# A macaron block with two routed expert layers on one core: expert products with the weights as the fixed side, and expert tiles sorted in one more class

## The chip, the cores and the metric

One core of one Trainium2 chip runs the whole program. The metric is the device time of the program in microseconds (us); the time of a kernel is the median of its runs.

## The reference, cut to what matters

2048 tokens (8 sequences of 256) with 128 features pass six stages, each added to what came in; all in float32. Stages one and three are the same expert layer:

```python
normed = _rmsnorm(x, norm_weight)                       # x is a layernorm of the stream
probs = softmax(normed @ router_weight.T)
topk_w, topk_idx = top_k(probs, 2); topk_w = topk_w / sum(topk_w)
for e in range(8):
    gate, up = split(normed @ gate_up_weight[e].T)      # 352 columns each
    out_e = (silu(gate) * up) @ down_weight[e].T
    moe_out = moe_out + combine[..., e, None] * out_e
return x + alpha * moe_out
```

Between them lies causal attention with 16 heads of 8. Behind them come a token-shift network (called mix here), a gated sum of nine shifted copies of the values (shift), and mix again.

## The kernel before, in words

The stream lies in SBUF as four tiles `x[0]` to `x[3]`, one for each group of 512 tokens (4 x 128 tokens on partitions, 128 features). All work is stated in Python as operations of the class `Work`: an engine, an estimated time, what it needs, and which buffers it takes and frees. `Work.issue` then places all of them by a list schedule and records each engine's instructions in that order, so the order on every engine is fixed by the planner's estimates and by the biases `BIAS` (added to the rank of late groups). `InOrder.issue` records each instruction, so nearly all of them show line 63 in the profile, and a register load shows line 72. Where the planner expects PE to idle, it places warming matmuls `pw`.

An expert layer (`moe_layer`) goes like this:

- `moe_route`, per group: normalise, store the rows to device memory (`rows0`, `rows1`), transpose, multiply by the router, take the top two (`topmost`).
- `moe_plan`, twice per layer: first over groups 0 and 1 alone, then over all groups. It counts tokens per expert with small matmuls and computes on DVE which row goes to which slot. There are 39 tiles of 128 slots; each tile has one expert. The first 9 tiles (`few`) are whole tiles of one expert filled from groups 0 and 1 alone; the 30 others come from the second plan. The plan leaves `take` (which row each slot fetches), `slot` (where a token's two results lie) and `expert` (the expert of each tile).
- `moe_experts` and `moe_tile`, per tile: POOL gathers 128 rows by an indirect DMA (`xs`), up to four tiles share a transpose `pt` and a scaled copy `nT`. PE reads the tile's expert into a register (`number`), then multiplies `nT` (the fixed side) with 352 columns of `gu` picked by the register, once for the gate (`pg`) and once for the up half (`pu`). ACT takes silu (`sg`), DVE multiplies (`hid`), PE transposes `hid` in three pieces (`ph`, at columns 0, 128 and 224: the list `HC`), ACT copies that (`hT`), and three matmuls with the expert's down weights add up to `po`. DVE copies it (`ys`), and SP stores it.
- `moe_back`, per group: for each of a token's two experts, four indirect DMAs on POOL fetch the results (`back`), and DVE adds them to `x`. Groups 0 and 1 may start once tiles 0 to 23 are stored; groups 2 and 3 once all 39 are.

All matmul results share eight PSUM banks (tag `b`). The attention's masks and constants (`mask_q`, `mask_k`, `va`, `mpad`, `onerow`) are made once the first layer's `affined` operation is done. In the second layer the end of the expert tiles is interleaved with mix of groups 0 and 1; shift and the last mix of all groups follow.

Of the kernel before, what the change touches and what calls it, by code (L numbers as in the profile page):

```python
# [19 lines left out]
P = 128  # L20
NG = 4
# [14 lines left out]
BIAS = (25.0, 30.0, 40.0, 55.0, 20.0, 2.0, -6.0)  # L36
# [181 lines left out]
def tile_macaron(ctx: ExitStack, tc: tile.TileContext, a: dict, out: bass.AP):  # L218
# [64 lines left out]
    with nc.allow_low_precision("zeros and ones"):  # L283
# [49 lines left out]
            "b": 8, "xs": 3, "nT": 3, "y": 2, "nTr": 1, "sg": 2, "hid": 2, "hT": 2, "ys": 4,  # L333
# [120 lines left out]
    def moe_layer(n, first):  # L454

        few = 2 * GT * first - 7
        r = {
            "n": n, "first": first, "few": few, "stored": {}, "all_stored": {}, "topped": {},
            "plan": {}, "hold": {},
        }  # L460
        for name, shape, dtype in (
            ("top", [P, NT, 8], F32), ("which", [P, NT, 8], U32), ("w", [P, NT, 2], F32),
            ("ab", [P, 2, NT], F32), ("rs", [P, NT], F32), ("slot", [P, 2 * NT], U32),
            ("take0", [P, few], U32), ("take1", [P, TILES - few], U32), ("expert", [1, TILES], I32),


            ("end", [P, E], F32), ("full", [P, 2, E], F32), ("base", [P, E], F32),
            ("both", [P, E], F32),
        ):
            r[name] = ctile(f"{name}_{n}", shape, dtype)  # L470
        for name, rows in (
            ("rows0", GT * first * P), ("rows1", NT * P), ("ys", TILES * P),
        ):
            r[name] = dram.tile([rows, P], F32, name=f"{name}_{n}", tag=f"{name}_{n}")
        return r

    def moe_route(g, r):
# [29 lines left out]
        tag = "nTr" if r["n"] else "nT"  # L507
        b1, b2, nTb = Buf("b"), Buf("b"), Buf(tag)
        pt = w.pe(0.44, lambda: transposed(filled[0].out), *filled, uses=[y], takes=[b1], spare=1)

        def scale_rows():
            nT = wtile(tag, "nT", (P, GT * P))
            nc.scalar.activation(
                nT, pt.out.rearrange("p t d -> p (t d)"), AF.Copy, scale=norm_w
            )
            return nT
# [85 lines left out]
    def moe_plan(r, whole):  # L602


        few = r["few"]
# [6 lines left out]
        def small(name, shape, dtype=F32):  # L612

            sizes = dict(zip("abc", shape[1:]))
            wide = 2 * NT * (TILES - 9)
            width = dict(
                oh=2 * NT * E, m=NT * E, slot=NT * E, past=2 * NT * E, sums=P, hit=wide, val=wide,
                le=3 * E, ef=1, eg=1, cb=E, nr=2 * E, at2=2 * E, up=2 * E,
                until=3 * E, whole=E,
            ).get(name, 2 * NT)  # L620
            rows = 1 if shape[0] == 1 else P
            room = wk.tile([rows, width], dtype, tag=name, name=name, bufs=1)
            n = 1
            for m in shape[1:]:
                n *= m
            v[name] = room[0 : shape[0], 0:n]
            if len(sizes) > 1:
                v[name] = v[name].rearrange(
                    f"p ({' '.join(sizes)}) -> p {' '.join(sizes)}", **sizes
                )  # L630
            return v[name]
# [34 lines left out]
        def place():  # L666

            sums = v["sums"]
            pp = bank([P, nt + 1, E], "pp")
            nc.tensor.matmul(  # L670
                pp[:, nt, :], lhsT=sums, rhs=same_e[0 : nt * E], start=True, stop=True
            )
            flat = pp.rearrange("p t e -> p (t e)")[:, 0 : nt * E]
            nc.tensor.matmul(flat, lhsT=before, rhs=v["m"], start=True, stop=False)
            nc.tensor.matmul(
                flat, lhsT=sums, rhs=earlier[0 : nt * E, 0:nt, :].rearrange("p t e -> p (t e)"),
                start=False, stop=True,
            )
            return pp
# [26 lines left out]
        def all_ends():  # L706
# [4 lines left out]
            left = small("cb", [P, E])  # L711
            nc.vector.tensor_tensor(left, placed.out[:, nt, :], full[:, 0, :], ALU.subtract)
            nc.vector.tensor_scalar(left, left, 63.5, 1.0 / P, ALU.add, ALU.mult)
            nc.vector.tensor_scalar(left, left, ROUND, ROUND, ALU.add, ALU.subtract)
            nr = small("nr", [P, 2, E])
            nc.vector.tensor_scalar(nr[:, 0, :], left, 1.0, None, ALU.min)
            nc.vector.tensor_tensor(nr[:, 1, :], left, nr[:, 0, :], ALU.subtract)

            until = small("until", [P, 3, E])
            nc.vector.tensor_copy(until[:, 0, :], r["end"])  # L720
            for k in range(2):
                nc.vector.tensor_tensor_scan(
                    until[:, k + 1, :], one8, nr[:, k, :], until[:, k, E - 1 : E], ALU.mult, ALU.add
                )


            at2 = small("at2", [P, 2, E])
            nc.vector.tensor_tensor(at2, until[:, 1:3, :], nr, ALU.subtract)
            up = small("up", [P, 2, E])
# [3 lines left out]
            nc.vector.tensor_tensor(up[:, 1, :], at2[:, 1, :], at2[:, 0, :], ALU.subtract)  # L733
            nc.vector.tensor_scalar(up[:, 1, :], up[:, 1, :], -1.0, float(P), ALU.add, ALU.mult)

        def all_slots():
            each, twice = [P, nt, E], [P, nt, 2, E]
# [3 lines left out]
                r["full"].unsqueeze(1).to_broadcast(twice), ALU.is_ge,  # L741
# [3 lines left out]
            nc.vector.tensor_tensor(past[:, :, 0, :], past[:, :, 0, :], past[:, :, 1, :], ALU.add)  # L745
            nc.vector.tensor_tensor(slot, slot, past[:, :, 0, :], ALU.add)

        ended = w.dve(2.4 if whole else 0.9, all_ends if whole else ends, placed, uses=[bp])
        spotted = w.dve(
            1.7 if whole else 0.75, all_slots if whole else slots, ended, uses=[bp]  # L750
# [73 lines left out]
        def which_expert():  # L824
# [3 lines left out]
            m = E * (3 if whole else 1)  # L828
# [34 lines left out]
    def moe_experts(r, sizes):  # L863


        stored, numbers, pus, turned, downs = [], {}, [], [], []
        k0 = 0
        for h in range(2):
            plan = r["plan"][h]
            rows = r["all_stored" if h else "stored"].values()  # L870
            for n in sizes[h]:
# [15 lines left out]
                for j in range(n):  # L887
                    got.append(w.pool(
                        0.98, lambda h=h, k=k0, j=j, f=gather: f(h, k, j), plan["taken"], *rows,
# [19 lines left out]
                for j in range(n):  # L909
                    stored.append(  # L910
                        moe_tile(r, plan, k0 + j, nT, nb, j, pus, turned, downs, numbers)
                    )
# [6 lines left out]
    def moe_tile(r, plan, k, nT, nb, j, pus, turned, downs, numbers):  # L919
        bg, bu, bh, bo = (Buf("b") for _ in range(4))  # L920
        sb, hb, tb, yb = Buf("sg"), Buf("hid"), Buf("hT"), Buf("ys")

        def number():
            numbers[k] = nc.tensor.value_load(
# [3 lines left out]
        known = w.pe(0.03, number, plan["experts"], *pus[-2:-1], lag=0.8)  # L928

        def product(c):  # L930
            wt = gu[:, bass.ds(numbers[k], 1), :].rearrange("p o h -> p (o h)")
            out = bank([P, HID], "pg" if c == 0 else "pu")
            nc.tensor.matmul(
                out, lhsT=nT.out[:, bass.ts(j, P)], rhs=wt[:, HID * c : HID * (c + 1)],
                start=True, stop=True,
            )
            return out

        pg = w.pe(0.6, lambda: product(0), known, nT, weights, *pus[-1:], *turned[-2:-1], *downs[-3:-2],
                  takes=[bg], uses=[nb], spare=3)  # L940
        pu = w.pe(0.6, lambda: product(1), pg, takes=[bu], uses=[nb])
        pus.append(pu)

        def gate():
            sg = wtile("sg", "sg", (P, HID))
# [7 lines left out]
        sg = w.act(0.47, gate, pg, takes=[sb], uses=[bg])  # L953

        def gated():
            hid = wtile("hid", "hid", (P, HID))
# [8 lines left out]
        hid = w.dve(0.53, gated, sg, pu, takes=[hb], uses=[sb, bu, bg])  # L965

        def turn():
            ph = bank([P, len(HC), P], "ph")
            for c, c0 in enumerate(HC):
                nc.tensor.transpose(ph[:, c, :], hid.out[:, c0 : c0 + P], ident)  # L970
            return ph

        ph = w.pe(0.34, turn, hid, takes=[bh], uses=[hb])
        turned.append(ph)

        def keep():
            hT = wtile("hT", "hT", (P, len(HC), P))
            nc.scalar.copy(hT, ph.out)
            return hT

        hT = w.act(0.48, keep, ph, takes=[tb], uses=[bh])

        def down():
            po = bank([P, P], "po")
            wt = dw[:, bass.ds(numbers[k], 1), :, :].rearrange("p o c d -> p (o c) d")
            for c in range(len(HC)):
                nc.tensor.matmul(
                    po, lhsT=hT.out[:, c, :], rhs=wt[:, c, :], start=(c == 0),
# [4 lines left out]
        po = w.pe(0.67, down, hT, takes=[bo], uses=[tb])  # L993
# [14 lines left out]
    def moe_back(g, r, stored):  # L1008
# [3 lines left out]
        until = 2 * GT * r["first"] + E if g < r["first"] else TILES  # L1012
# [10 lines left out]
        for c in range(2):  # L1023
# [3 lines left out]
            def gather(t, c, box=box):  # L1027
                if t == 0:
# [9 lines left out]
                    0.98, lambda t=t, c=c, f=gather: f(t, c), plan["slots"], *stored[:until],  # L1038
# [21 lines left out]
    def attention(begun):  # L1060
# [6 lines left out]
        def constants(mask, step):  # L1067
# [8 lines left out]
            w.pool(1.3, lambda m=m, step=step: constants(m, step), begun)  # L1076
# [8 lines left out]
            ), begun,  # L1085
# [3 lines left out]
            [w.pool(1.4, lambda v=v: nc.gpsimd.memset(v[:, :, :, DK:32], 1.0), begun)] for v in va  # L1089
# [3 lines left out]
            [[w.pool(0.5, lambda m=m: nc.gpsimd.memset(m, 0.0), begun)] for m in row]  # L1093
# [550 lines left out]
    outs = attention(r0["hold"][0]["affined"])  # L1644
# [94 lines left out]
```

## Time and profile before

| what | value |
|---|---|
| median of 5 runs | 588.6 us (588.47 to 595.54) |
| profiled execution, its own time | 590.61 us |
| its span | 588.9 us |
| mean granted clock of PE | 0.933 |
| busy: PE, weight loads, DVE, ACT, POOL | 514.4, 363.8, 320.4, 253.7, 229.2 us |

The profile is of one execution. PE is TensorE, PEld its weight loads (they overlap its matmuls), DVE is VectorE, ACT ScalarE, POOL GpSimd, SP the engine that issues plain DMAs. In the slices, each digit is the busy share of a fortieth of the span in tenths, and PEclk the granted clock in tenths. A row of the groups has the busy time and the mean of one instruction, then the idle time of the engine ahead of it and what ended it ("issue" is a wait for nothing that the profile shows, "remote" one for an unknown source). A row of the timeline has the start, the length, the engine and the operation. A row of the windows has the stretch, its length, then busy time (and instructions) of PE, PEld, DVE, ACT and POOL, the granted clock, the DMA share and GB/s. Ends of matmuls are modelled.

In time: loading, routing and the first plan of layer one to about 34 us; its tiles to about 176, the last of them beside attention, which runs from about 131 to 335; the tiles of layer two from 335 to 484; then the back-gathers and the tail of shift and mix to 589.

### The profile page before, as it was taken

To read this page: it belongs to the slowest core of one execution; us is meant where nothing else is said; L and a number is where in the kernel's file an instruction comes from. 1 tells how busy PE (TensorE), PEld (TensorE's weight loads), DVE (VectorE), ACT (ScalarE), POOL (GpSimd) and SP (SyncE) were. 2 spreads that over 40 slices of the span, in tenths; PEclk is the share of its full clock that TensorE was granted. 3 is DMA by queue.
4 is the path that set the end of the run, shared out by engine and by line. 5 is a ranking of instruction groups with operands and counts; after the bars stand their busy time and mean duration, and the time that the engine had idled before them with its cause. 6 is when DMAs were issued, how large, how long until landed. Compare 5 with 4: busy or idle time off the path is not lost.

```text
span 588.9 us, 12554 instructions
## 1 busy us (share of the span) xinstructions
PE 514.4 (87%) x4619; PEld 363.8 (62%) x4619; DVE 320.4 (54%) x1139; ACT 253.7 (43%) x536; POOL 229.2 (39%) x239
## 2 busy tenths in 40 slices
PE   7869599887997899999998799597985999699985
PEld 3447478655774666776776575475764774466574
DVE  7676144245853586777772378132323344479891
ACT  3223166324153246456444350255332646164653
POOL 4231679553005500000004202666255037777651
PEclk9879699988998899999999798898999799799998
DMA  8721222221001100000100010212312001100001
GB/s 288 242 82 37 58 55 55 59 52 35 19 20 37 32 7 2 3 20 4 56 2 26 16 46 10 69 45 60 45 55 59 14 24 42 30 0 2 1 19 55
DMA packets 27036, 26.26 MB, mean 45 GB/s; under 512 B 4064, under 2 KB 24288, under 8 KB 26560
## 3 DMA queue, kind: packets, MB, share of 16 engines
q1 hardware_dynamic: 21232, 15.60, 8.5%
q0 software_dynamic: 4544, 9.32, 6.5%
q8 instruction: 39, 0.64, 0.5%
q10 hardware_dynamic: 1200, 0.53, 0.3%
q14 instruction: 21, 0.17, 0.1%
HBM read 17.18 MB, written 9.31 MB: 45 GB/s over the span
## 4 chain that ended last, share of the span: by engine, by line
PE 52%; issue 8%; POOL 7%; DVE 7%; ACT 3%; another core or an unknown queue 2%; DMA 1%; POOLq 0%; DVEq 0%; ACTq 0%
PE sc L63 16%; PE po L63 10%; PE pu L63 5%; PE pg L63 5%; PE pt L63 3%; POOL back L63 3%; PE ph L63 3%; PE pr L63 2%; POOL q L63 2%; PE pm L63 1%; PE pw L63 1%; PE pv L63 1%; POOL x L63 1%; DVE stats L63 1%
## 5 line engine op out<-in xcount | busy, mean ns | idle before, releaser
L63 POOL DMA_INDIRECT xs<-rows,take x78 | 74.9, 961 | 138.4 <-DVE take L63 41.8
L63 PE MATMUL po<-dw,hT 128*128 x468 | 72.1, 295 | 32.2 <-issue 19.5
L63 PEld LDWEIGHTS po<-dw,hT 128*128 128x128 f32 x468 | 66.9, 205 | 52.3 <-issue 26.1
L63 POOL DMA_INDIRECT back<-ys,slot x64 | 61.1, 954 | 75.4 <-DMA ys<-ys 35.6
L63 DVE TENSOR_TENSOR hid<-sg,pu 128x352 f32<-128x352 f32 x78 | 40.5, 520 | 83.5 <-PE pu L63 41.4
L63 ACT ACTIVATE ep<-sc 128x512 f32<-128x512 f32 x96 | 52.2, 596 | 67.4 <-PE sc L63 55.4
L63 ACT COPY hT<-ph 128x384 f32<-128x384 f32 x78 | 37.3, 478 | 88.5 <-PE ph L63 44.0
L63 POOL TENSOR_TENSOR stats<-stats,minus_half 128x4 f32<-128x4 f32 x28 | 28.6, 1023 | 113.1 <-DVE stats L63 112.7
L63 PE MATMUL pg<-gu,nT 128*128 x156 | 65.4, 503 | 0.5 <-ACT nT L63 0.5
L63 PE MATMUL pu<-gu,nT 128*128 x156 | 63.3, 489 | 0.0
L63 PE MATMUL sc<-qT,kT 32*128 32x128 f32 x768 | 59.2, 290 | 2.5 <-issue 1.3
L63 PEld LDWEIGHTS sc<-kT,qT 32*128 32x128 f32 x768 | 47.8, 191 | 19.5 <-issue 17.6
L63 PE MATMUL sc<-kT,qT 32*128 32x128 f32 x768 | 57.5, 290 | 0.0
L63 ACT ACTIVATE sg<-pg 128x352 f32<-128x352 f32 x78 | 36.0, 463 | 49.5 <-PE pg L63 32.5
L63 DVE TENSOR_REDUCE mtmp<-sc 128x4 f32<-128x512 f32 x64 | 41.5, 686 | 23.5 <-PE sc L63 20.6
L63 PEld LDWEIGHTS sc<-qT,kT 32*128 32x128 f32 x768 | 49.4, 191 | 5.0 <-issue 3.5
L63 DVE COPY ys<-po 128x128 f32<-128x128 f32 x78 | 22.1, 288 | 47.8 <-PE po L63 23.1
L63 PE MATMUL ph<-ident,hid 128*128 128x128 f32 x234 | 40.5, 286 | 2.5 <-issue 1.8
L63 PEld LDWEIGHTS ph<-ident,hid 128*128 128x128 f32 x234 | 30.7, 148 | 16.1 <-issue 9.6
L63 PE MATMUL pw<-before,ones_b 128*128 128x512 bf16 x119 | 31.5, 413 | 7.0 <-DVE p L63 4.5
L63 PE MATMUL pgt<-yTg,rest 128*128 128x512 f32 x72 | 33.4, 597 | 0.3 <-ACT yTg L63 0.2
L63 PEld LDWEIGHTS pu<-gu,nT 128*128 128x128 f32 x156 | 27.9, 204 | 8.1 <-issue 2.1
(197 smaller groups left out, 887.5 us busy)
## 6 DMA issues: line engine op xcount, KB each, us to landing
ys<-ys SPq DMA_DIRECT2D x78, 64.0 KB
gu<-in_guT SPq DMA_DIRECT2D x2, 1408.0 KB
rest<-in_rest SPq DMA_DIRECT2D x1, 1280.0 KB
xs<-rows,take POOLq DMA_INDIRECT x78
x<-in_x SPq DMA_DIRECT2D x4, 256.0 KB
dw<-in_dwT SPq DMA_DIRECT2D x1, 1024.0 KB
rows<-rows SPq DMA_DIRECT2D x2, 512.0 KB
back<-ys,slot POOLq DMA_INDIRECT x64
```

What stands on the lines that cost most here:

```text
L63: ins = do(*args, **kw)
```

## The change

- *The fixed side.* The tile's expert number is now also loaded into registers of ACT and DVE. ACT copies the expert's gate weights (128 x 352, `wg`) and DVE its up weights (`wu`) to fixed places, two buffers each. PE takes 128 columns of the copy as the fixed side and `nT`'s 128 tokens as the moving side, three times per product, so that `pg`, `pu`, `sg` and `hid` hold inner rows on partitions (3 x 128 with an overlap of 32) and `hid` is the fixed side of the down product at once. `ph` and `hT` go, with one bank per tile.
- *Order of the tiles.* In layer two (`soon` = 3) the second plan sorts its tiles in three classes instead of two: one tile per expert, then those that groups 0 to 2 still fill, then the rest. Group 2's back-gathers need the tiles up to 32.
- *Planner.* Gathers are stated at 1.25 us instead of 0.98; `BIAS` is new; the attention's constants wait for nothing; the second layer's `nT` of the router shares the tiles' buffers; the plan's `val` shares room with `past`.

```diff
-BIAS = (25.0, 30.0, 40.0, 55.0, 20.0, 2.0, -6.0)
+BIAS = (35.0, 17.0, 32.0, 26.0, 27.0, 12.0, -6.0)
...
     def moe_layer(n, first):
         few = 2 * GT * first - 7
+        soon = first + 1 if n == 1 and first + 1 < NG else None
...
     def moe_plan(r, whole):
-        few = r["few"]
+        few, soon = r["few"], r["soon"] if whole else None
+        parts = 3 if soon else 2
...
+            if soon:
+                rows = slice(0, GT * soon * E)
+                nc.tensor.matmul(
+                    pp[:, nt + 1, :], lhsT=sums[rows, :], rhs=same_e[rows], start=True, stop=True
+                )
...
+            if soon:
+                nc.vector.tensor_tensor(nr[:, 2, :], left[:, 0, :], nr[:, 0, :], ALU.subtract)
+                nc.vector.tensor_scalar(nr[:, 1, :], left[:, 1, :], -1.0, 0.0, ALU.add, ALU.max)
+                nc.vector.tensor_tensor(nr[:, 2, :], nr[:, 2, :], nr[:, 1, :], ALU.subtract)
+                nc.vector.scalar_tensor_tensor(
+                    full[:, 2, :], nr[:, 1, :], float(P), full[:, 1, :], ALU.mult, ALU.add
+                )
...
-            for k in range(2):
+            for k in range(parts):
                 nc.vector.tensor_tensor_scan(
...
                     got.append(w.pool(
-                        0.98, lambda h=h, k=k0, j=j, f=gather: f(h, k, j), plan["taken"], *rows,
+                        1.25, lambda h=h, k=k0, j=j, f=gather: f(h, k, j), plan["taken"], *rows,
...
-        known = w.pe(0.03, number, plan["experts"], *pus[-2:-1], lag=0.8)
+        late = pus[-2:-1]
+        known = w.pe(0.03, lambda: number("tensor"), plan["experts"], *late, lag=0.8)
+        for_gate = w.act(0.06, lambda: number("scalar"), plan["experts"], *late)
+        for_up = w.dve(0.06, lambda: number("vector"), plan["experts"], *late)
+
+        def copied(c):
+            name, engine = (("wg", "scalar"), ("wu", "vector"))[c]
+            dst = wtile(name, name, (P, HID))
+            src = gu[:, bass.ds(held[engine], 1), :].rearrange("p o h -> p (o h)")
+            src = src[:, HID * c : HID * (c + 1)]
+            if c == 0:
+                nc.scalar.copy(dst, src)
+            else:
+                nc.vector.tensor_copy(dst, src)
+            return dst
+
+        wg = w.act(0.45, lambda: copied(0), for_gate, weights, takes=[wgb])
+        wu = w.dve(0.45, lambda: copied(1), for_up, weights, takes=[wub])
+
+        def product(name, weight):
+            out = bank([P, len(HC), P], name)
+            for c, c0 in enumerate(HC):
+                nc.tensor.matmul(
+                    out[:, c, :], lhsT=weight.out[:, c0 : c0 + P],
+                    rhs=nT.out[:, bass.ts(j, P)], start=True, stop=True,
+                )
             return out
-        pg = w.pe(0.6, lambda: product(0), known, nT, weights, *pus[-1:], *turned[-2:-1], *downs[-3:-2],
-                  takes=[bg], uses=[nb], spare=3)
-        pu = w.pe(0.6, lambda: product(1), pg, takes=[bu], uses=[nb])
+        pg = w.pe(
+            0.67, lambda: product("pg", wg), wg, nT, *pus[-1:], *downs[-2:-1], takes=[bg],
+            uses=[nb, wgb], spare=2,
+        )
+        pu = w.pe(0.67, lambda: product("pu", wu), wu, pg, takes=[bu], uses=[nb, wub])
...
-        ph = w.pe(0.34, turn, hid, takes=[bh], uses=[hb])
-        hT = w.act(0.48, keep, ph, takes=[tb], uses=[bh])
...
-                    po, lhsT=hT.out[:, c, :], rhs=wt[:, c, :], start=(c == 0),
+                    po, lhsT=hid.out[:, c, :], rhs=wt[:, c, :], start=(c == 0),
...
-        until = 2 * GT * r["first"] + E if g < r["first"] else TILES
+        until = TILES
+        if g < r["first"]:
+            until = 2 * GT * r["first"] + E
+        elif r["soon"] and g < r["soon"]:
+            until = 2 * GT * r["soon"] + E
...
-    outs = attention(r0["hold"][0]["affined"])
+    outs = attention()
```

## The prediction

> **What bounds the kernel now.** I read the page's slices first, then the groups, then TensorE's timeline in a calm stretch, and last the queues beside each idle stretch of TensorE.
>
> ```profile
> PE   7869599887997899999998799597985999699985
> PEclk9879699988998899999999798898999799799998
> ```
>
> TensorE (PE) is nearly full in most of the 40 slices; where its digit falls, the granted clock falls in the same slice or the next.
>
> ```profile
> L63 PE MATMUL po<-dw,hT 128*128 x468 | 72.1, 295 | 32.2 <-issue 19.5 <-ACT hT L63 9.1 <-ACT nT L63 3.1
> L63 PE MATMUL pg<-gu,nT 128*128 x156 | 65.4, 503 | 0.5 <-ACT nT L63 0.5
> L63 PE MATMUL pu<-gu,nT 128*128 x156 | 63.3, 489 | 0.0
> L63 DVE TENSOR_TENSOR hid<-sg,pu 128x352 f32<-128x352 f32 x78 | 40.5, 520 | 83.5 <-PE pu L63 41.4 <-ACT sg L63 13.8 <-remote 10.4
> L63 PE MATMUL ph<-ident,hid 128*128 128x128 f32 x234 | 40.5, 286 | 2.5 <-issue 1.8 <-DVE hid L63 0.7
> L63 ACT COPY hT<-ph 128x384 f32<-128x384 f32 x78 | 37.3, 478 | 88.5 <-PE ph L63 44.0 <-remote 22.0 <-PE po L63 7.5
> ```
>
> The 78 expert tiles are 241 us of PE's 514 busy. What one costs is read from starts, since ends are modelled:
>
> ```profile
> 87.62 0.76 PE L63 MATMUL pu<-gu,nT 128*128 x2
> 88.21 0.49 PE L63 MATMUL ph<-ident,hid 128*128 128x128 f32 x3
> 88.54 0.76 PE L63 MATMUL pg<-gu,nT 128*128 x2
> 89.14 0.76 PE L63 MATMUL pu<-gu,nT 128*128 x2
> 89.73 0.83 PE L63 MATMUL po<-dw,hT 128*128 x6
> 90.39 0.49 PE L63 MATMUL ph<-ident,hid 128*128 128x128 f32 x3
> ```
>
> From start to start: pu 0.59, ph 0.33, pg 0.60, po 0.66, together 2.18 us; pt adds 0.11. Here PE sets the pace. Elsewhere it does not:
>
> ```profile
> 371.32 0.49 PE L63 MATMUL pt<-ident,xs 128*128 128x128 f32 x3
> 378.06 1.22 PE L63 MATMUL po<-dw,hT 128*128 x4 [6.25 <-issue]
> 372.69 0.94 POOL L63 DMA_INDIRECT xs<-rows,take  x1 [0.30 <-issue]
> 373.94 0.94 POOL L63 DMA_INDIRECT xs<-rows,take  x1 [0.30 <-issue]
> ```
>
> PE idles 6.25 us while GpSimd issues gathers without a pause, one every 1.25 us (ten from 363.86 to 376.13). The runs 55 to 67, 110 to 121, 399 to 409, 432 to 442 and 445 to 455 look alike. In such a run the trace's events show PE's signals to ACT and DVE 2 to 3 us apart (60.75, 62.91, 65.74, 68.61), though its matmuls had issued; in calm stretches they follow each matmul. PE's idle stretches among the tiles come to 13.6 us in the first expert layer (1.20, 4.06, 1.22, 1.03, 0.85, 2.12, 0.63, 2.52) and 20.0 in the second (6.25, 2.15, 1.35, 0.69, 2.36, 1.22, 6.01). Two more places are not PE's:
>
> ```profile
> 363.39 0.19 DVE L63 TENSOR_SCALAR take<-pi 128x30 uint32<-128x30 f32 x1
> 486.32 1.02 POOL L63 DMA_INDIRECT back<-ys,slot  x1 [0.34 <-issue]
> 507.35 0.94 POOL L63 DMA_INDIRECT back<-ys,slot  x1 [0.30 <-issue]
> 480.00:510.00 30.00, 24.62 (x99) 12.54 (x98) 11.63 (x43) 14.02 (x33) 22.19 (x23) 0.95 0.14 42
> ```
>
> The second layer's plan ends on DVE at 363.4, and its 30 late tiles can't be gathered before. After the last tile (ys at 483.3) 16 back-gathers hold POOL from 486.3 to 508.3, with q sums between them, and the last two groups start behind them.
>
> **The change, part by part** (sums against this execution's 590.6 us, 2.0 over the median of 588.6).
>
> *Products.* pg and pu become three matmuls of 128 columns each, the shape of po: 0.66 a product. ph goes. A tile: 3 x 0.66 = 1.98 against 2.18, so -0.20. The first nine tiles of a layer run while the plan is made and gain nothing, since what follows waits for the plan; 2 x 30 tiles gain: **-12.0**. Bounds: 0 (hand-overs bind) and 78 x 0.20 at the mean clock 0.93, -16.8. The Trainium skill (TensorE: Matmul & The Clock Gate, "Back-to-back issue gap") speaks against it: a matmul of 128 columns with a weight load of its own sustains about 81 ns, not 56. At two passes a record that estimates 6 x 0.162 = 0.97 us a product, 2.9 a tile, and a loss of some 43 us over 60 tiles; po's six records in 0.66, weight loads included, say otherwise.
>
> *Copies.* ACT loses hT (0.478) and gets wg, 352 columns from SBUF: between sg (0.463) and ka (0.628 for 512), say 0.50. DVE gets wu: between ys (0.288 for 128) and va (0.690 for 512), and at 352 next to hid, 0.52. hid and sg grow by 32 columns, 0.03 each. ACT and DVE each get a register load per tile; the nearest row is PE's:
>
> ```profile
> L72 PEldq TENSOR_LOAD <-expert x78: 297/300/493, 32.5 to 471.2; - x78
> ```
>
> With the register work around it (0.07 each, from the trace) 0.45 us, or nothing where the engine is still busy. ACT per tile: 0.50 + 0.49 + 0.17 (nT) + 0.45 = 1.6; DVE: 0.52 + 0.55 + 0.29 + 0.45 = 1.8. PE needs 2.09 with pt, so PE covers them in the calm stretches: 0. Cover gone, a wait of up to 0.45 a tile, +27. wg and wu have two buffers and wait in ACT's and DVE's queues for products two tiles back; sg, hid and ys stand behind them, and PE waits for those. Against that, a PE-to-ACT round (ph, hT) leaves the chain. In the gather runs, where such signals are late, one crossing of three goes but copies now wait too: from a third of 33.6 (-11) to +8; I take **-2**.
>
> The Trainium skill (SBUF — State Buffer, "SBUF: two separate sides") warns that an fp32 copy inside SBUF on DVE locks GpSimd out, so that its gathers can't write descriptors. The nearest row is y (TENSOR_SCALAR, 16 of them): eight ran beside gathers at 337 to 417 ns, eight without at 340 to 349. By the row it costs nothing; if by the rule a quarter of the copies waited half a gather (0.47), it would be an estimated 9 us of DVE.
>
> *Plans.* First layer: seven copies, eight loads and six hid stand on DVE ahead of take, five ys less: 7 x 0.52 + 8 x (0 to 0.45) - 5 x 0.28 = 2.2 to 5.8, of which some 3.5 us of idle gaps between 38 and 54.6 take most: 0 to 3, I take **+1.5**. Second layer, DVE unbroken from 344 to 363: about one copy and one ys more before the marks (0.8), two loads (0.6), two copies and a ys beyond the wait for pp (1.0), eight small operations for the third class of tiles (0.17 to 0.29 each) with wider past (1.5), and the expert numbers now ahead of take (0.4): **+4.3**, 2 to 6.
>
> *Third class of tiles.* Group 2 needs ys up to tile 32 instead of 39, so 8 of the 16 last gathers move ahead of the last tile. POOL after it is freed of 8 x 1.25 = 10 us; the last two groups share DVE (27.5 of 30 us in 540 to 570), so I count **-8** (0 to -10). The eight gathers now run on beside expert tiles: a run of eight cost 2.4 to 6 us of PE idle, some of it after the work there is done: **+3** (0 to 6).
>
> *The rest.* The masks and constants (6.0 us of POOL, from 84 to 101) move to the start, where POOL idles 8.8 us before 20.4: 0; cover gone, +2. Gather prices and biases only move order: 0, within 3 either way.
>
> Sum: -12.0 - 2 + 1.5 + 4.3 - 8 + 3 = -13.2. 590.6 - 13.2 = 577.4 for a profiled run, 575.4 against the median; I say **576**, with 568 to 584 as this case's own range.
>
> **Rivals.**
> *Hand-overs bind* (slower). DVE's 1.8 and ACT's 1.6 are near PE's 2.09, and both queues stand still at each copy that waits for a product. The place is sg and hid behind a load and a copy; it decides once about 0.2 us a tile shows. At 0.35 x 60 = +21 against -13: +8, near 597. For it: hid already waits 41 us for pu, and loads are bare where an engine idles. Against: ACT was busy 14.7 and DVE 10.2 of 30 us in 90 to 120.
> *Gain hidden.* Where gather runs and plans set the pace a faster tile waits longer: without the -12 the sum is -1.2, 587. For it: 33.6 us of PE idle. Against: full slices.
> *Stalls shrink.* One crossing less ends a third of the 33.6 (-11 instead of -2) and a third of the clock lost behind them (windows of 30 us at 0.83, 0.83, 0.89 and 0.89 from 60, 360, 390 and 450: 17 us; -6): 577.4 - 9 - 6 - 2 = 560.4, 560.
> *Only the order moves*: if the third class did not free group 2 earlier, the -8 and +3 fall away: 581, inside the forecast.
>
> **How the numbers follow.** Forecast 0.45, hand-overs 0.22, hidden 0.18, stalls shrink 0.15. A measurement here tells about 1% (6 us) from no change. Nearly all of the forecast and the shrunken stalls are faster: 0.60; slower is the hand-over case and a little: 0.23; the same 0.17. The range 560 to 597 takes in the forecast, the hidden case and the nearer half of the other two.
>
> **What would show it.** pg and pu at 0.66 from start to start and 2.0 a tile in calm stretches; no ph; wu near 0.52; take of the second layer 4 us later after its routing; eight gathers after the last ys. I am wrong if PE waits for hid or wg in calm stretches, if wu or its load stretches beside gathers, or if the idle in gather runs grows.

## The result, and the profile after

The changed kernel took 596.8 us (median of 39 runs, 593.4 to 600.9) against 592.2 for the kernel before (76 runs, 586.9 to 602.1) in the same measurement: a ratio of 1.0095, interval 1.008 to 1.0111. It is 1% slower; the prediction of 576 us said 2% faster (576 against 588.6). The profiled execution has a span of 594.2 us.

First the slices and the groups of the page after, for the lines that the prediction shows of before:

```profile
PE   8868589858997989999988999858987879899995
PEclk9779789979998799999995999779998899999999
L63 PE MATMUL po<-dw,hid 128*128 x468 | 73.1, 297 | 42.3 <-DVE hid L63 32.3
L63 DVE TENSOR_TENSOR hid<-sg,pu 128x384 f32<-128x384 f32 x77 | 42.3, 552 | 64.2 <-remote 19.4
L63 PE MATMUL pg<-nT,wg 128*128 128x128 f32 x468 | 72.5, 295 | 2.3 <-ACT nT L63 0.7
L63 PE MATMUL pu<-nT,wu 128*128 128x128 f32 x468 | 69.8, 289 | 0.0
L63 ACT COPY wg<-gu 128x352 f32 x78 | 37.4, 485 | 13.0 <-ACT sg L63 4.6
L63 DVE COPY wu<-gu 128x352 f32 x78 | 27.6, 354 | 22.1 <-issue 8.1
```

ph and hT are gone; pg and pu are now 468 records each. PE's idle time ahead of po has grown from 32.2 to 42.3 us, and what ends it is now hid. TensorE's timeline in a calm stretch, and the register loads (minimum, median and longest in ns):

```profile
98.84 0.84 PE L63 MATMUL pg<-nT,wg 128*128 128x128 f32 x6
99.52 0.83 PE L63 MATMUL pu<-nT,wu 128*128 128x128 f32 x6
100.19 0.84 PE L63 MATMUL po<-dw,hid 128*128 x6
100.87 0.83 PE L63 MATMUL pg<-nT,wg 128*128 128x128 f32 x6
```

```profile
L72 ACTq TENSOR_LOAD <-expert x78: 272/278/571, 31.5 to 479.0; - x78
L72 DVEq TENSOR_LOAD <-expert x78: 298/303/549, 31.6 to 483.4; - x78
```

From start to start 0.68, 0.67 and 0.68: a tile takes 2.03 us where it took 2.18, near the forecast's 1.98. The gain is there, and the kernel is slower all the same. The windows of the expert tiles' two stretches, from the plan's take to the last ys, first of before and then of after (stretch, length, then busy time and instructions of PE, PEld, DVE, ACT and POOL, granted clock, DMA share, GB/s):

```profile
54.60:174.50 119.90, 104.86 (x706) 78.77 (x706) 52.96 (x152) 48.90 (x106) 58.47 (x62) 0.93 0.17 45
363.40:483.30 119.90, 99.57 (x545) 76.02 (x546) 39.88 (x143) 50.12 (x114) 57.45 (x56) 0.90 0.19 45
```

```profile
54.50:177.90 123.40, 102.27 (x868) 91.00 (x872) 64.17 (x194) 49.73 (x103) 52.72 (x52) 0.92 0.18 46
377.40:491.70 114.30, 89.27 (x668) 82.92 (x669) 51.45 (x185) 43.62 (x95) 63.54 (x62) 0.91 0.20 52
```

PE's idle time there (length less busy) went from 15.0 + 20.3 = 35.4 us to 21.1 + 25.0 = 46.2. Where it lies, a stretch of the timeline of after beside eight back-gathers (439 to 449 us) shows:

```profile
440.32 0.49 ACT L63 ACTIVATE sg<-pg 128x384 f32<-128x384 f32 x1 [0.85 <-PE pg L63]
440.99 0.48 ACT L63 COPY wg<-gu 128x352 f32 x1 [0.17 <-issue]
441.46 0.83 PE L63 MATMUL pg<-nT,wg 128*128 128x128 f32 x6
442.13 0.83 PE L63 MATMUL pu<-nT,wu 128*128 128x128 f32 x6
445.38 0.94 PE L63 MATMUL po<-dw,hid 128*128 x6 [2.41 <-issue]
446.58 0.91 PE L63 MATMUL pg<-nT,wg 128*128 128x128 f32 x6 [0.26 <-issue]
447.71 0.94 POOL L63 DMA_INDIRECT back<-ys,slot  x1 [0.30 <-issue]
450.43 0.49 ACT L63 ACTIVATE sg<-pg 128x384 f32<-128x384 f32 x1 [8.96 <-remote]
450.96 0.55 DVE L63 TENSOR_TENSOR hid<-sg,pu 128x384 f32<-128x384 f32 x1 [5.04 <-ACT sg L63]
451.09 0.48 ACT L63 COPY wg<-gu 128x352 f32 x1 [0.17 <-ACT sg L63]
451.56 1.61 PE L63 MATMUL po<-dw,hid 128*128 x6 [4.08 <-DVE hid L63]
```

The pg that starts at 441.46 is done by 442.3, but the sg that reads it starts at 450.43. The trace's events have PE's signals at 440.30, 444.68 and 450.41 in this stretch; behind the waiting sg stands the next tile's wg, and behind that the next pg. PE idles 2.4 and 4.1 us, and both times its next work is a po that waits for hid. Elsewhere ACT waits in the same way: in the waits of after (us in total, times, longest), sg behind a releaser that the profile can't name, and PE behind hid:

```profile
ACT sg L63 <- remote: 40.5, 5, 11.0
PE po L63 <- DVE hid L63: 32.3, 15, 7.3
```

The second layer's take came at 377.4 instead of 363.4. Of these 14 us the plan itself is 3 (16.2 us from the routing's last operation to take before, 19.2 after); the rest came before it, in attention, whose last score ended at 337.7 instead of 319.7. From the last ys of the first layer to that score attention took 159.8 us instead of 145.2. So between these two executions it is attention that grew most, while the two stretches of tiles together are 2.1 us shorter. Layer two's run of nine gathers began 4 us before the last score in before (315.9); in after it lies among the scores (306.4 to 316.5). PE's signals are 7.2 us apart there (312.19 to 319.42), PE idles 4.6 of 20 us, and the granted clock is 0.69 and 0.63:

```profile
307.90:317.90 10.00, 6.76 (x46) 4.00 (x44) 2.37 (x5) 1.46 (x3) 7.39 (x8) 0.69 0.19 54
317.90:327.90 10.00, 8.68 (x112) 5.93 (x112) 4.65 (x9) 5.11 (x11) 0.00 (x0) 0.63 0.02 7
```

### The profile page after: what moved, and what is told of

It reads as the page before. It is cut to its first block, busy times and chain, and to the rows that moved or that the text cites. A ratio compares the mean times of both kernels' runs of the same rounds, so it can differ in the third digit from the quotient of the medians.

```text
span 594.2 us, 13952 instructions
## 1 busy us (share of the span) xinstructions
PE 513.6 (86%) x5044; PEld 397.7 (67%) x5044; DVE 344.8 (58%) x1225; ACT 258.2 (43%) x536; POOL 229.8 (39%) x239
## 4 chain that ended last, share of the span: by engine, by line
PE 65%; DVE 12%; issue 7%; another core or an unknown queue 6%; DMA 5%; POOL 2%; ACT 2%; DVEq 0%; ACTq 0%; POOLq 0%; SPq 0%
PE sc L63 16%; PE po L63 12%; PE pg L63 8%; PE pu L63 7%; PE pt L63 5%; PE pgt L63 4%; PE pw L63 3%; DVE x L63 2%; PE pv L63 2%; DMA rows<-n 2%; PE pr L63 2%; DVE st L63 2%; PE pm L63 1%; DVE hid L63 1%
## 5 line engine op out<-in xcount | busy, mean ns | idle before, releaser
L63 PE MATMUL po<-dw,hid 128*128 x468 | 73.1, 297 | 42.3 <-DVE hid L63 32.3
L63 PEld LDWEIGHTS po<-dw,hid 128*128 128x128 f32 x468 | 63.3, 206 | 48.0 <-DVE hid L63 34.9
L63 ACT ACTIVATE sg<-pg 128x384 f32<-128x384 f32 x78 | 38.1, 489 | 126.4 <-PE pg L63 56.6
L63 DVE TENSOR_TENSOR hid<-sg,pu 128x384 f32<-128x384 f32 x77 | 42.3, 552 | 64.2 <-remote 19.4
L63 PE MATMUL pg<-nT,wg 128*128 128x128 f32 x468 | 72.5, 295 | 2.3 <-ACT nT L63 0.7
L63 PE MATMUL pu<-nT,wu 128*128 128x128 f32 x468 | 69.8, 289 | 0.0
L63 PEld LDWEIGHTS pg<-nT,wg 128*128 128x128 f32 x468 | 64.4, 209 | 5.2 <-ACT nT L63 2.3
L63 PEld LDWEIGHTS pu<-nT,wu 128*128 128x128 f32 x468 | 63.3, 205 | 0.8 <-ACT qT L63 0.8
L63 PEld LDWEIGHTS sc<-qT,kT 32*128 32x128 f32 x768 | 51.2, 197 | 10.0 <-issue 8.9
L63 ACT COPY wg<-gu 128x352 f32 x78 | 37.4, 485 | 13.0 <-ACT sg L63 4.6
L63 DVE COPY wu<-gu 128x352 f32 x78 | 27.6, 354 | 22.1 <-issue 8.1
```

The lines of the kernel that those rows point to most:

```text
L63: ins = do(*args, **kw)
```

## The experiments

### The same two kernels on other chips

The first four experiments ran on a chip where before took 535.7 us, not 592. So both kernels were run as they are.

> The changed kernel as it is, beside the same runs of before as the three that follow. In the first experiments before ran in 535.7 us, not 592, and PE's signals followed its matmuls through runs of 18 gathers; there a_bias stood at 0.976 and a_tile at 0.96 of before. If such a chip is drawn again: theory B (only the late signals beside gathers made the change slow) expects the change to be faster here, 0.96 to 0.985 of before; theory A (biases) expects 0.985 to 1.0, slower than a_bias by 6 to 10 us; if before is near 590 again, 1.005 to 1.015, as on record.

> The kernel before, for its profile on this chip. If before is near 535 us: PE idle among the expert tiles under 8 us instead of the 33.6 of the profile shown, no signals of PE more than 1.5 us apart beside gathers while its matmuls issue, and calm tiles of 2.18 us as before. If it is near 590: as in the profile shown.

On chip 3 before took 535.0 us (17 runs) and the change stood at 0.958 of it (0.9526 to 0.9635): 511.0 us, 4% faster. The run labelled before2 stood at 1.0025 (0.9987 to 1.0064). In all, before took 533 to 536 us on chips 3, 4, 6, 9 and 14, and 584 to 586 on chips 7 and 10; chips 3 and 7 came up twice and were of the same kind both times. No median lies between. I call the two kinds prompt and late, because of this: the timeline of after2 on chip 3, in the middle of a run of 13 gathers:

```profile
375.90 0.84 PE L63 MATMUL pg<-nT,wg 128*128 128x128 f32 x6
376.43 1.04 POOL L63 DMA_INDIRECT back<-ys,slot  x1 [0.30 <-issue]
376.57 0.83 PE L63 MATMUL po<-dw,hid 128*128 x6
376.77 0.49 ACT L63 ACTIVATE sg<-pg 128x384 f32<-128x384 f32 x1 [0.87 <-PE pg L63]
377.24 0.83 PE L63 MATMUL pu<-nT,wu 128*128 128x128 f32 x6
377.44 0.48 ACT L63 COPY wg<-gu 128x352 f32 x1 [0.17 <-ACT sg L63]
377.77 0.94 POOL L63 DMA_INDIRECT back<-ys,slot  x1 [0.30 <-issue]
377.91 0.83 PE L63 MATMUL pg<-nT,wg 128*128 128x128 f32 x6
```

The same instructions with the same durations, the same gathers, here 1.25 to 1.4 us apart; but the sg starts 0.87 us after its pg, and PE's signals come 0.67 us apart while its expert matmuls issue. Neither of the two waits shown above is among the sixty longest of after2. The windows of the expert tiles say what it is worth, of before2 and of after2:

```profile
56.00:163.90 107.90, 101.63 (x706) 77.28 (x707) 53.72 (x152) 49.03 (x105) 58.52 (x62) 0.97 0.21 50
331.50:430.90 99.40, 94.71 (x546) 73.47 (x547) 40.23 (x144) 50.37 (x114) 57.38 (x56) 0.94 0.25 55
```

```profile
52.20:148.80 96.60, 92.82 (x868) 83.46 (x872) 64.35 (x194) 49.95 (x103) 53.32 (x52) 1.00 0.25 58
321.80:408.80 87.00, 84.26 (x677) 78.64 (x678) 52.26 (x184) 44.28 (x95) 63.15 (x62) 0.96 0.29 68
```

Lengths of the stages in us, PE's idle time in brackets:

| stage | before, late | before2, prompt | after, late | after2, prompt |
|---|---|---|---|---|
| to the first layer's take | 54.6 | 56.0 | 54.5 | 52.2 |
| its late tiles | 119.9 (15.0) | 107.9 (6.3) | 123.4 (21.1) | 96.6 (3.8) |
| attention, to the last score | 145.2 (6.7) | 133.4 (1.6) | 159.8 (11.5) | 133.4 (0.4) |
| to the second layer's take | 43.7 (6.8) | 34.2 (1.5) | 39.7 (2.9) | 39.6 (2.9) |
| its late tiles | 119.9 (20.3) | 99.4 (4.7) | 114.3 (25.0) | 87.0 (2.7) |
| tail | 105.6 | 106.3 | 102.5 | 99.5 |
| span | 588.9 | 537.2 | 594.2 | 508.3 |

On the late chip before takes 51.7 us more of span than on the prompt one, and the changed kernel 85.9, nearly all of it in stages in which PE works beside runs of gathers. Between these executions the change gains 28.9 us on a prompt chip and loses 5.3 on the record's. That the late signals are the cause is read from the traces, in which PE's idle time and the lower clock stand beside them; no run ends them on a late chip with all else as it was. The 11.0 us of PE's idle time among the tiles of before2 are more than the 8 expected.

### The expert tile alone

```diff
 # a_tile, a_tile_2: the changed kernel with moe_tile of before
...
-        wg = w.act(0.45, lambda: copied(0), for_gate, weights, takes=[wgb])
-        wu = w.dve(0.45, lambda: copied(1), for_up, weights, takes=[wub])
...
+        ph = w.pe(0.34, turn, hid, takes=[bh], uses=[hb])
...
+        hT = w.act(0.48, keep, ph, takes=[tb], uses=[bh])
 # b_tile, b_tile_2: the reverse, on before (and the router's nT in the tiles' buffers)
```

> The changed kernel with the expert tile of before (rows of tokens as the fixed side, ph and hT, no copies wg and wu), all else as changed: three classes of tiles, biases, price of gathers, early constants. Theory A: the tile itself gains in its place (2.02 us a tile instead of 2.18 in calm stretches, 60 tiles), so that taking it back costs up to 10 us while the late plan stays: 600 to 606. Theory B: PE's idle time in the two stretches of expert tiles (21.1 and 25.0 us in the changed kernel, 15.0 and 20.3 before) falls back by about 11 us, which pays for the dearer tile: 594 to 599. Theory C: between the two.

> The kernel before with the new expert tile alone (weights as the fixed side, copies wg and wu, register loads on ACT and DVE; the router's nT shares the tiles' buffers as in the change), with the biases, the price of gathers, the two classes and the late constants of before. Theory A: the tile's gain shows, less 1.5 us in the plans: 580 to 585. Theory B: PE's idle beside the gather runs grows by 8 to 12 us and eats the gain: 589 to 594. In both the second layer's take is late by no more than 4 us against before.

> The changed kernel beside a_tile_2, to weigh the new expert tile alone inside the new order. Theory T1 (the tile pays where PE sets the pace): 60 tiles by 0.16 us, less one wait or another, so 4 to 10 us faster than a_tile_2. Theory T2 (what the tile saves on PE is waited for elsewhere, on GpSimd's gathers, attention and the plan): within 3 us of a_tile_2. Where before is near 590: late signals rule, and it stands at 1.005 to 1.015 of before.

> The changed kernel with the expert tile of before once more, on one chip with after3. T1: 4 to 10 us slower than after3; T2: within 3 us of it. Where before is near 590, the chain with ph and hT meets late signals less often with its longer queue of work ahead: 5 us or more faster than after3 if the new tile is what made the change slow there, slower than after3 if the order is.

> The kernel before with the new expert tile alone, again (1.011 where before took 535.7). Where before takes 585 or more: if the new tile's hand-overs meet late signals worse, 1.01 to 1.025, and PE's idle among the tiles is above 33.6 us; if only the new order does, 0.99 to 1.005. Where before takes 535: 1.0 to 1.015 again.

| | prompt chip | late chip |
|---|---|---|
| change with the old tile (a_tile, a_tile_2) | 0.960 (0.9522 to 0.9678) | 0.997 (0.9933 to 1.0008) |
| change (after2, after3) | 0.958 (0.9526 to 0.9635) | 1.0167 (1.0111 to 1.0222) |
| before with the new tile (b_tile, b_tile_2) | 1.0106 (1.0032 to 1.018) | 1.0273 (1.0171 to 1.0375) |

The ratios are to before on the same chip. On the late chip 7 the new tile costs 2% in the new order (1.0167 against 0.997, run together: 0.0197 x 584.8 = 11.5 us), and on chip 10 2.7% in the old one (16 us). On prompt chips it makes no difference that these intervals show in the new order, and costs 1% in the old one. With the old tile the new order loses nothing on a late chip, so the tile decides there; 1.0167 and 1.0273 are a little worse than expected (up to 1.015 and 1.025). The planner places all work anew for each kernel, however, so a variant differs from its neighbour in the order on every engine too, and what that alone is worth is not separated. The windows of b_tile_2:

```profile
55.20:175.30 120.10, 100.44 (x864) 90.38 (x866) 67.31 (x196) 49.76 (x103) 58.83 (x62) 0.93 0.19 47
374.70:493.10 118.40, 94.69 (x692) 89.54 (x693) 50.35 (x171) 50.53 (x109) 57.24 (x56) 0.89 0.19 46
```

Idle 19.7 + 23.7 = 43.4 us among the tiles, near the 46.2 of after, against 35.4 with the old tile in the profile of before. The pair that ran on one chip, 7, shows the same, first a_tile_2, then after3:

```profile
51.20:175.40 124.20, 106.56 (x711) 78.55 (x710) 52.09 (x154) 49.05 (x105) 52.71 (x52) 0.92 0.18 43
375.30:484.80 109.50, 92.60 (x497) 70.07 (x498) 40.21 (x152) 43.02 (x98) 63.05 (x63) 0.89 0.22 53
```

```profile
54.20:175.90 121.70, 98.98 (x868) 87.28 (x872) 64.22 (x194) 49.18 (x103) 52.84 (x52) 0.96 0.19 46
372.70:485.40 112.70, 90.62 (x665) 83.12 (x666) 51.80 (x184) 44.10 (x95) 63.09 (x62) 0.89 0.21 53
```

The stretches are as long with the new tile as with the old (234.4 us against 233.7): PE is busy 9.6 us less and idles 10.3 us more (44.8 against 34.5). The gain of the faster tile is waited away. Where the 11.5 us of loss lie these two traces do not show: their spans are only 2.4 us apart, since that of a_tile_2 is its longest run (587.3 us against a median of 581.9).

On prompt chips, in the new order, PE idles 3.8 and 2.7 us in after2, and the tile stretches are 183.6 us long against 189.0 with the old tile (a_tile): 5.4 of the forecast 12 us. Some of the rest may be the 18 more warmers that the planner places (153 pw against 135, at 0.22 us from start to start: 4 us); that is not shown. In the old order idle time does grow there, from 11.0 us in before2 to 17.4 in b_tile.

### The order alone

```diff
 # a_bias (on the change; b_bias is the reverse, on before)
-BIAS = (35.0, 17.0, 32.0, 26.0, 27.0, 12.0, -6.0)
+BIAS = (25.0, 30.0, 40.0, 55.0, 20.0, 2.0, -6.0)
 # a_nosoon (on the change)
-        soon = first + 1 if n == 1 and first + 1 < NG else None
+        soon = None
 # a_price (on the change; b_price is the reverse, on before), both gathers
-                        1.25, lambda h=h, k=k0, j=j, f=gather: f(h, k, j), plan["taken"], *rows,
+                        0.98, lambda h=h, k=k0, j=j, f=gather: f(h, k, j), plan["taken"], *rows,
```

> The changed kernel with the six planner biases of before, all else as changed. Theory A (attention stage): the 14 us by which layer two's second plan is late (take at 377.4 us instead of 363.4) come from the biases, which put layer two's early routing and a run of nine gathers (306 to 317 us) between attention scores that last to 337.5. Then the run of nine moves behind the last score again, take falls to about 366 to 369, and the time by 7 to 10 us, to about 587. Theory B (hand-overs in gather runs): what was lost lies beside the gather runs of the expert tiles, which the biases do not touch: within 3 us of the changed kernel, 594 to 600. Theory C (no single cause, each order has its own luck): anything within 6 us, with idle moved from one place to another.

> The changed kernel with two classes of tiles again: group 2's back-gathers need all 39 tiles. As the prediction has it the third class is worth 8 at the tail, less 3 for an extra run of gathers beside tiles and about 2.5 in the second plan: 2 to 6 us slower than the changed kernel. Rival: without late signals the extra run beside tiles costs nothing and the tail sets the end, so 8 us slower. Rival: the tail is bound by DVE and PE anyway, so within 2 us.

> The kernel before with the new biases alone. Theory A: its second layer's routing and a run of gathers move among the attention scores, and it loses 4 to 10 us against before. Theory C: biases only choose among orders of about equal worth, within 4 us either way. If the biases are what a_tile gained with (0.96 of before with the old tile), 10 to 20 us faster.

> The kernel before, in which the planner takes 1.25 us for a gather instead of 0.98 (a gather starts every 1.25 us in every trace); all else as before. On the chips where before takes 535 us the whole change stood at 0.958, without the third class at 0.9725, with the biases of before at 0.976 and with the expert tile of before at 0.96, and the biases alone or the tile alone at 1.007 and 1.011. Theory C1 (the stated price of a gather is what these need: a plan of the order that matches the gathers): 0.975 to 0.99 of before by itself. Theory C2 (none of the parts gains alone, only together): 0.995 to 1.01. If before is near 590 here, late signals beside gathers rule and I expect 0.99 to 1.01.

> The changed kernel with gathers stated at 0.98 us again, all else as changed. By itself the price of 1.25 brought before to 0.988. Where before takes 535: if the price is a part of the gain of its own, 0.965 to 0.98 of before (the change: 0.958); if it only goes with the old biases, within 0.5% of the change. Where before takes 585 or more: 1.005 to 1.03, since gathers that are thought shorter are lined up in no longer runs but PE's work is planned closer behind them.

On prompt chips: a_bias 0.9762 (0.9687 to 0.9837), a_nosoon 0.9725 (0.967 to 0.978), b_bias 1.007 (1.0034 to 1.0105), b_price 0.9878 (0.98 to 0.9957), against 0.958 for the change. So the 4% are the planner's and the third class's: the class is worth 1.5% (8 us), the biases 1.8% in the new order and less than nothing in the old, the stated price of 1.25 us 1.2% by itself. On the late chip 7 a_price stood at 1.0332 (1.0267 to 1.0397), the change with the price at 1.0167. So the price is worth 1.6% there too; the reason that I gave for it is not shown by the trace. a_nosoon lost the 8 us of its first rival, b_price came out as C1 had it, and a_price is just above its range. My theory A for the late take (the biases) was not decided: both runs on biases fell on prompt chips, where attention took 133 to 135 us with either set. On late chips it took 161.6 us in a_tile_2 (old tile, new order) and 154.0 in b_tile_2 (new tile, old order), against 145.2 in before, each on another late chip, so neither alone accounts for it.

### Runs of gathers broken into fours

```diff
+    def landed(last):
+        if gone["n"] == 4:
+            nc.gpsimd.tensor_copy(seen, gone["last"])
+            gone["n"] = 0
+        gone["n"], gone["last"] = gone["n"] + 1, last
...
+                    landed(box["xs"][:, j, 0:1])
                     i = k + j - h * r["few"]
...
+                landed(box["back"][:, t, 0:1])
                 at = NT * c + GT * g + t
 # a_drain4, b_drain4: gathers stated at 1.8; a_break4, at_break4: at 1.25, the change's own order
```

> The changed kernel, in which GpSimd reads one column of the latest gathered block after every four gathers, so that it waits for their landing before it issues the fifth; gathers are stated at 1.8 us. If PE's idle stretches come from runs of more than four gathers on GpSimd (PE's signals come 3 to 6 us apart from about the fifth on: 440.30, 444.68, 450.41), the two idle pieces in each run (2.4 and 4.1 us beside 439 to 449) shrink to under 1 us, PE's idle in the stretches of tiles falls from 46 to under 25 us, and the time by 12 us or more, to 575 to 585. If they come from copies and loads that wait in ACT's and DVE's queues, the idle stays and the waits for landings add 3 to 10 us: 597 to 607.

> The kernel before, in which GpSimd waits after every four gathers for their landing before it issues the fifth (gathers stated at 1.8 us). Where before takes 585 or more, and PE's late signals come from more than four gathers in a row: PE's idle beside gathers (33.6 us among the tiles) falls below 15 and the time to 0.95 to 0.985 of before; if lateness does not depend on the length of the run, 1.0 to 1.04. Where before takes 535: the waits alone, 1.03 to 1.06 (a_drain4 stood at 1.053 of before, where the change without them stands at 0.958).

> The changed kernel in its own order, with GpSimd waiting after every four gathers for their landing (the price of a gather stays 1.25 us, so that nothing else moves). Where before takes 585 or more: late signals are gone, 0.95 to 0.98 of before, and within 1% of at_break4 or faster than it, if the late signals are what makes the new tile dear; 1.01 to 1.02 times at_break4 if the tile is dear for another reason. Where before takes 535: the waits alone, 1.0 to 1.04 of before.

> The changed kernel with the expert tile of before and the same waits after every four gathers. Where before takes 585 or more: 0.955 to 0.985 of before (the old tile lost less to late signals, so it wins less by their end). Where before takes 535: 1.0 to 1.04.

> The changed kernel with GpSimd waiting after every four gathers (stated at 1.8 us), once more. Where before takes 585 or more: as b_drain4 lost only 7% of its time there against undisturbed chips, and the waits set the time on both kinds, 555 to 572 us, 0.95 to 0.98 of before, where the change without them stood at 1.0167; if the new tile is dear there for a reason other than late signals, 0.99 to 1.01. Where before takes 535: 1.045 to 1.06 again.

> The changed kernel in its own order with waits after every four gathers, once more. Where before takes 585 or more: 0.95 to 0.985 of before if late signals are what the change loses by there (against 1.0167 without the waits); 1.0 to 1.03 if not. Where before takes 535: 1.045 to 1.065 again.

Of the six, only b_drain4 fell on a late chip (10). There it stood at 0.9887 of before (0.9783 to 0.9991), though on prompt chips such waits bring the change from 0.958 to 1.0535 (1.0457 to 1.0612) and 1.0488 (1.0437 to 1.0538), and without a new price to 1.055 (1.0462 to 1.0637) and 1.0534 (1.0476 to 1.0592). The start of one four of b_drain4 in the timeline, TensorE and GpSimd:

```profile
364.35 0.18 POOL L63 COPY seen<-xs 128x1 f32<-128x1 f32 x1 [1.65 <-DMA xs<-rows,take]
364.79 0.76 PE L63 MATMUL pu<-gu,nT 128*128 x2
365.00 0.97 POOL L63 DMA_INDIRECT xs<-rows,take  x1 [0.47 <-issue]
365.39 0.49 PE L63 MATMUL ph<-ident,hid 128*128 128x128 f32 x3
365.71 0.76 PE L63 MATMUL pg<-gu,nT 128*128 x2
366.28 0.94 POOL L63 DMA_INDIRECT xs<-rows,take  x1 [0.30 <-issue]
```

Its windows of the tiles:

```profile
53.70:168.80 115.10, 109.92 (x721) 79.65 (x721) 52.35 (x155) 50.10 (x106) 60.24 (x73) 0.99 0.20 49
350.30:440.60 90.30, 86.67 (x501) 65.24 (x502) 33.67 (x111) 40.54 (x90) 51.03 (x60) 0.97 0.24 58
```

PE idles 5.2 + 3.6 us, against 35.4 in the profile of before from another late chip, at a clock of 0.99 and 0.97; the idle time is under the 15 us expected, the ratio a little above the 0.95 to 0.985. This is not all the signals' doing: the higher price made the planner place 66 warmers in these stretches (16 us of PE); without them PE would idle some 22.7 us, with two pieces over 2 us instead of seven. Nor are late signals gone. Beside one four (357.97 to 365) the longest gap between PE's signals is 2.1 us, against 4.4 at the same place of before, but beside others it is 4.7 (from 61.94), 4.0 (from 91.95) and 3.0 (from 373.20), though PE's matmuls had issued. So b_drain4 is the one kernel on a late chip whose interval lies below before; but it changes the waits, the price, the order and the warmers together, and what each is worth is open.

at_break4 stood at 1.0758 (1.0661 to 1.0856) beside a_break4's 1.055 on the prompt chip 9: with the runs broken, and on a prompt chip, the new tile is 2% (11 us) faster than the old. Both are above the 1.0 to 1.04 that were expected of the waits. Whether the new tile gains so on a late chip is open, since neither ran on one.

## Why the prediction was wrong, step by step

- *A tile at 0.66 a product*: right, 0.67. The Trainium skill (TensorE: Matmul & The Clock Gate, "Back-to-back issue gap") gives about 81 ns for a matmul of 128 columns with its own weight load; the estimate of 0.97 us a product made from it, with two passes a record, is not borne out: six records with their own weight loads start 0.67 us apart from the next six.
- *Copies and loads cost nothing*: right in the calm stretches. wg took 0.485 (0.50 said), wu 0.354 (0.52 said: too dear), the loads 0.28 and 0.30 with 0.15 and 0.19 of register work. Beside gathers wu took 0.363 us in the mean and 0.347 alone, and a gather 967 ns beside such a copy and 958 alone (median 944 both). The lock of which the Trainium skill warns (SBUF — State Buffer, "SBUF: two separate sides") cost next to nothing here: 0.016 us a copy.
- *Hand-overs in the gather runs, -2 with -11 to +8*: **the step that failed.** I saw the late signals and then reasoned that one crossing less would pay for two copies that wait. PE's idle time among the tiles grew by 10.8 us, past the upper bound; in b_tile_2, in the order of before, by 8.0; between a_tile_2 and after3, on one chip, by 10.3. That ate the 9.6 us that PE was busy less. The tile's part of the sum was -12 - 2 + 1.5 = -12.5; on chip 7 it measured +11.5 (after3 against a_tile_2). These 24 us are the whole miss there (1.0167 instead of 576 / 588.6 = 0.9786 is 22 us), but of the 11.5 the waits among the tiles explain only why nothing was gained; where the loss beyond that lies is open. Why the new tile meets late signals worse is open too. It is not that pg and pu wait for their copies: PE's idle time ahead of pg is 2.3 us and ahead of pu 0.0 in all of after, and 42.3 ahead of po, which waits for hid. That PE has less work in its queue behind the last prompt signal is argued from one place each: before still had 3.7 us (368.13 to the end of pt at 371.8), after 2.7 (440.30 to the end of pu at 443.0).
- *The miss by stage*, on the record's chip (18.5 us between the two profiled executions and the sum): tiles -11 forecast (-12, -2 and +3), -2.1 measured; attention and the second plan +4.3 forecast, +10.6 measured; tail -8 and -3.1; to the first take +1.5 and -0.1. So the waits among the tiles are half of it, and attention, to which I gave nothing, is the next part.
- *-12 from 60 tiles* as a term of its own: not shown in these kernels. On a late chip PE is busy 9.6 us less but waits as much more; on a prompt one the tile stretches are 5.4 us shorter. With waits after every four gathers, on the prompt chip 9, the new tile gained 11 us (a_break4 against at_break4).
- *Plans*: the first +1.5, measured -0.1 (54.6 to 54.5); by the tile alone on chip 7, +3.0 (51.2 in a_tile_2, 54.2 in after3). The second +4.3 (2 to 6), measured +3.0, of which 1.8 for the third class (19.2 us against 17.4 in a_nosoon).
- *Third class, -8 at the tail and +3 for the extra run*: with 1.8 in the plan the net forecast was -3; on a prompt chip the class gains 8 us in all (a_nosoon); on the record's the tail fell by 3.1. The eight gathers after the last ys are there (495 to 505).
- *Biases and price, 0 within 3*: wrong in size. They are worth 6 to 10 us each way: price 1.2% on a prompt chip and 1.6% on a late one, biases 1.8% in the new order. All order changes together (a_tile_2) came to -0.3% on a late chip, near the -1 of my sum (-8 + 3 + 4.3), so this did not decide the result there.
- *Rivals*: "hand-overs bind" had the number (597) and, in part, the place. It put the price into every tile, 0.35 us behind a load and a copy; calm tiles show none of it (2.03 us); the waiting is in the gather runs. "Stalls shrink" was the opposite of what happened.

## What to carry to other kernels

When the trace shows a resource that already disturbs one stage (here a signal that arrives late beside runs of gathers), do not credit a change there for the crossings that it removes: in three comparisons the idle time grew by 8 to 11 us with a crossing less. A time saved on the busiest engine is a gain only in stretches in which that engine waits for nobody; measure those apart first. And compare kernels on the same chip: here two kinds of chip reverse the verdict (0.958 and 1.0167).

## What the runs showed of the hardware

- The same program runs 9 to 11% apart on different chips (533 to 536 us on five, 584 to 586 on two, 592 in the measurement of the result), with equal busy time of DVE, ACT and GpSimd (320.4, 253.7 and 229.2 us in before, 321.6, 253.9 and 229.2 in before2) and equal pitch of the gathers (1.25 us). The traces differ in when PE's signals arrive beside GpSimd's back-to-back indirect gathers: 0.67 us apart on chip 3, up to 7.9 us apart on the record's chip (from 61.37 in after). There the gaps begin behind the first to fifth gather of a run (4.4 us from 440.30 in after, behind the second; 4.4 from 368.13 in before, behind the fourth), and in short runs too (3.8 us from 421.45 in before, in a run of four). The expectation of a_drain4, that they begin at about the fifth, read the trace too narrowly. What makes a chip late is open.
- The granted clock falls to a half in single stretches (311.7 to 325.4 us in after) and is lower where PE idles: in the tiles' two stretches it is 0.92 and 0.91 in after, with 46.2 us of idle time, and 1.00 and 0.96 in after2, with 6.5.
- A wait of GpSimd for the landing after four gathers (1.65 us in the line shown) did not end the late signals: in b_drain4 gaps of 3.0 to 4.7 us remain beside runs of four.
